# A graph layer on one core: 139 gathered columns and 15 single rows a chunk in place of 35 columns

## The chip, the cores and the metric

One core of a Trainium2 chip runs the whole program. The metric is device time in microseconds, the median of several executions; smaller is better. The figures that follow are from one profiled execution (its span is 4845.3 us, its own time 4847.12 us) unless they are called a median.

## The reference

A message-passing layer over 12500 nodes (48 features) and 400000 edges (32 features), the edges sorted by their target `dst`:

```python
h = jnp.maximum(_layernorm(x, axis=-1), 0.0)
x_i, x_j = h[dst], h[src]
tmp = jnp.concatenate([x_i, x_j, edge_attr], axis=1)       # 48 + 48 + 32
hid = jax.nn.relu(tmp @ W1 + b1)                            # 128 wide
msg = hid @ W2 + b2
out = x + jax.ops.segment_sum(msg, dst, num_segments=12500)
```

`dst` is sorted, `src` is random. That makes the target part of each edge's input local, and the source part a gather.

## The kernel before, in words

**Set-up** (the first 140 us or so). `node_tables` computes the normalised nodes and three tables: `tab_a` (nodes times the target rows of W1, with b1, in DRAM), `tab_b` (nodes times the source rows of W1, in DRAM, one row of 128 floats for each node), and `bt`, the transpose of `tab_b`, which stays in SBUF: 128 partitions, one column for each node.

**Chunks.** The edges are cut into 3125 tiles of 128 edges, eight tiles to a chunk, 391 chunks (`NCH`). The loop over the chunks is written out in full, and `manual_schedule` keeps each engine's instructions in the order in which the code names them. For chunk c:

- `prepare(c)`: SP loads the 80 rows of `tab_a` that the chunk's targets span (`rhs`), the edge features (`lhs`) and the targets (`row`). POOL gathers a row of `tab_b` for each edge into `gb`, one indirect DMA for each tile (`gathered_at`). There are six buffers `gb`, so POOL can run up to six chunks ahead; it then waits for DVE to have read the oldest. DVE builds two one-hot matrices, `lhs` (target by edge) and `hot` (edge by target).
- `before(c)`: PE multiplies `lhs` by `rhs` into `pre` in PSUM: the target part and the edge part of the hidden layer, eight tiles.
- `hidden(c)`: DVE adds `gb` to `pre` and writes `hid` in SBUF; ACT applies the relu.
- `fold(c)`: PE multiplies `hid` by `hot` into `p_g`; `add(c)`: DVE adds that into the running segment `seg`.

An iteration of the loop runs `prepare(c)`, `before(c-1)`, `fold(c-2)`, `turned(c-1)`, `hidden(c-1)` and `add(c-2)`. Every 12 chunks a segment is multiplied by W2 and stored.

**Columns in place of gathers.** Some tiles are not gathered by POOL. For these, ACT and DVE copy the edges' columns of `bt` one by one into a tile `gt` (128x128), each from an address that stands in a register (`columns`); PE adds the transpose of `gt` into `pre` (`turned`). The numbers come from the table `last`: `load` issues one TENSOR_LOAD for up to 32 registers. `PARTS` says which engine makes how many columns a chunk, and where their numbers lie in the table. Before the change DVE makes 3 and ACT twice 16, so 35 a chunk: a tile of 128 columns is full every 3.66 chunks, 106 tiles of 3125 in all, and 3019 tiles are left to POOL.

```python
PARTS = (
    (True, 0, 3, 1),
    (False, 3, 16, 4),
    (False, 19, 16, 20),
)
```

Of the kernel before, what the change touches and what calls it, by code (L numbers as in the profile page):

```python
# [8 lines left out]
F32 = mybir.dt.float32  # L9
I32 = mybir.dt.int32  # L10
AF = mybir.ActivationFunctionType
# [5 lines left out]
P = 128  # L17
N, D, DE, HID, E = 12500, 48, 32, 128, 400000
# [3 lines left out]
NT = E // P  # L22
T = 8
# [20 lines left out]
U8 = mybir.dt.uint8  # L44
# [3 lines left out]


COLS = 1  # L50
END = NT // T


PARTS = (
    (True, 0, 3, 1),
    (False, 3, 16, 4),
    (False, 19, 16, 20),
)
PART = sum(n for _, _, n, _ in PARTS)
BASE = 36  # L60
DVE_PARTS = sum(dve for dve, *_ in PARTS)
BEHIND = len(PARTS) - 1

BT0 = 16512
SEG0 = 121888
SEG_SIZE = 8 * L


SEG, NEXT, SEG2 = 40, 41, 42
PLACE0 = 43  # L70
WIDTH = 44
SLOTS = (NCH + 2 + P - 1) // P
MOST = 32

# [1 line left out]
def tiles_of(first, part):  # L76

    n = (END - first) * part // P
    return [first + (P * (j + 1) + part - 1) // part - 1 for j in range(n)]


BYCOLS = tiles_of(COLS, PART)
TURNED = {c: [j for j, of in enumerate(BYCOLS) if of == c] for c in set(BYCOLS)}


def turned_at(c):

    return ((), (T - 1,), (T // 2 - 1, T - 1))[len(TURNED.get(c, ()))]


def gathered_at(c):

    return [t for t in range(min(T, NT - c * T)) if t not in turned_at(c)]


EPS = 1e-5
# [151 lines left out]
def windows(nc, tc, gp, bt, ident, idx, x_t, tab_a, tab_b, dst, edge_t, w1, w2s, b2s, out_t):  # L248
# [3 lines left out]
    with ExitStack() as es:  # L252
# [5 lines left out]
        gtp = es.enter_context(tc.tile_pool(name="gtp", bufs=5))  # L258
        wp = es.enter_context(tc.tile_pool(name="wp", bufs=3))
# [12 lines left out]
        for _, _, n, at in PARTS:  # L272
# [1 line left out]
                last[:, :, at : at + n], last[:, :, at : at + n], 4, BT0,  # L274
                op0=ALU.mult, op1=ALU.add,
            )
        rows_at = slice(BASE, BASE + 1)
        nc.vector.tensor_scalar(
            last[:, :, rows_at], last[:, :, rows_at], 4 * HID, None, op0=ALU.mult
        )  # L280
        taba8 = tab_a.rearrange("n h -> (n h)").bitcast(U8)

        place = PARTS[0][3] - 1
        for a, b in ((place, SEG2), (NEXT, SEG)):
# [5 lines left out]
        nc.vector.scalar_tensor_tensor(  # L290
            last[:, :, at_place], last[:, :, at_place], 4.0, last[:, :, PLACE0 : PLACE0 + 1],
            op0=ALU.mult, op1=ALU.add,
# [8 lines left out]
            rhss.append(rhs)  # L301
        st = {}
        gts = {}

        def group(c):

# [5 lines left out]
        def numbers(c, at, n, engine):  # L312

            got = []
            for k in range(0, n, MOST):
                got += nc.values_load_multi_w_load_instructions(  # L316
                    last[c % P : c % P + 1, c // P, at + k : at + min(k + MOST, n)],
                    engines=[engine], min_val=0, max_val=1 << 23,
                    skip_runtime_bounds_check_because="numbers of nodes, and what is made of them",
                )[1]  # L320
            return got

        def node(n):
            return n.with_bounds(min_val=0, max_val=N - 1)

        regs = {}

        def load(c, part):

            dve, first, n, at = PARTS[part]  # L330
            n = max(0, min(n, len(BYCOLS) * P - ((c - COLS) * PART + first))) if c >= COLS else 0
            engine = mybir.EngineType.DVE if dve else mybir.EngineType.Activation
# [7 lines left out]
        def columns(c, part):  # L340
# [3 lines left out]
            for k, at in enumerate(regs.pop((c, part), [])):  # L344
                of, e = divmod((c - COLS) * PART + first + k, P)
                if of not in gts:
# [6 lines left out]
        def prepare(c):  # L353
            n = min(T, NT - c * T)
            at = c * CE
            base, = numbers(c, BASE, 1, mybir.EngineType.SP)
            rhs = rhss[c % 3]
            base = base.with_bounds(min_val=0, max_val=4 * HID * (N - 1))
            nc.sync.dma_start(
                rhs.bitcast(U8)[:W, :],  # L360
                taba8[bass.ds(base, 4 * HID * W)].rearrange("(w h) -> w h", w=W),
            )
            lhs = ld.tile([P, CE], F32, name="lhs")
            nc.sync.dma_start(lhs[W:K, : n * P], edge_t[:, at : at + n * P])
            row = ld.tile([W, CE], I16, name="row")
            nc.sync.dma_start(
                row[:, : n * P],
                dst[at : at + n * P].rearrange("(o e) -> o e", o=1).to_broadcast([W, n * P]),
            )
            st[c] = dict(n=n)  # L370
            gb = gp.tile([P, T, HID], F32, name="gb")
            for t in gathered_at(c):
                nc.gpsimd.indirect_dma_start(  # L373
                    out=gb[:, t, :], out_offset=None, in_=tab_b[:, :],
                    in_offset=bass.IndirectOffsetOnAxis(
                        ap=srci[:, c * T + t : c * T + t + 1], axis=0
                    ),
                )

            deg = degs[c % 3]  # L380
            nc.vector.tensor_scalar(  # L381
                lhs[:W, : n * P], row[:, : n * P], bw[:, c : c + 1], None,
                op0=ALU.is_equal, op1=ALU.add, accum_out=deg[:, :1],
            )
            load(c, 0)
            columns(c, 0)
            hot = wp.tile([P, T, W], F32, name="hot")
            nc.vector.tensor_tensor(  # L388
                hot[:, :n, :], wnum.unsqueeze(1).to_broadcast([P, n, W]),
                rel[:, c * T : c * T + n].unsqueeze(2).to_broadcast([P, n, W]), op=ALU.is_equal,  # L390
            )
            st[c].update(rhs=rhs, lhs=lhs, gb=gb, deg=deg, hot=hot)
# [18 lines left out]
        def hidden(c):  # L411
            s = st[c]
            n, pre = s["n"], s["pre"]
            h = wp.tile([P, T, HID], F32, name="hid")
            two = len(turned_at(c)) == 2
            half = T // 2

            def added(x, to):

                if not two:  # L420
                    return x[:, :to, :]
                return x.rearrange("p (b t) h -> p b t h", b=2)[:, :, : half - 1, :]

            to = n - len(turned_at(c))
            nc.vector.tensor_add(added(h, to), added(pre, to), added(s["gb"], to))  # L425
            if two:
                nc.scalar.activation(
                    h[:, half - 1 :: half, :], pre[:, half - 1 :: half, :], AF.Relu
                )
            elif to < n:  # L430
                nc.scalar.activation(h[:, to, :], pre[:, to, :], AF.Relu)  # L431
            nc.scalar.activation(added(h, to), added(h, to), AF.Relu)  # L432
            s["h"] = h

        def fold(c):
# [10 lines left out]
        def add(c):  # L446

            s = st.pop(c)
            k = group(c)[0] % 2
            of = SEG0 + k * SEG_SIZE  # L450
            at = s["base"].with_bounds(
# [37 lines left out]
        with tc.manual_schedule():  # L489
            for c in range(NCH + 2):  # L490
                if c < NCH:
                    prepare(c)
                if c >= NCH:
                    load(c, 0)
                    columns(c, 0)
                for part in range(1, DVE_PARTS - 1):
                    load(c, part)
                    columns(c, part)
                if 0 <= c - 1 < NCH:
                    before(c - 1)  # L500
                if 0 <= c - 2 < NCH:
                    fold(c - 2)
                if 0 <= c - 1 < NCH:
                    turned(c - 1)

                g, k = group(c - 2)
                if k == GQ - 3 or c == NCH - 1:
                    segment_load(g)
                if g > 0 and k < L // BLK:
                    segment_sum(g - 1, k, BLK)  # L510
                if g > 0 and k == STORE:
                    segment_store(g - 1, L)
                columns(c, DVE_PARTS)
                for part in range(DVE_PARTS + 1, BEHIND):
                    load(c, part)
                    columns(c, part)
                if 0 <= c - 1 < NCH:
                    hidden(c - 1)
                if DVE_PARTS > 1:
                    load(c, DVE_PARTS - 1)  # L520
                for part in range(BEHIND, len(PARTS)):
                    load(c, part)
                    columns(c, part)
                load(c + 1, DVE_PARTS)
                if 0 <= c - 2 < NCH:
                    add(c - 2)
                    if k == GQ - 1:
                        segment_next(g)
                if DVE_PARTS > 1:
                    columns(c, DVE_PARTS - 1)  # L530
                if c == NCH + 1:
                    segment_sum(g, 0, END_L)
                    segment_store(g, END_L)

                if c < PIECES:
                    s = slice(c * PIECE, (c + 1) * PIECE)
                    nc.sync.dma_start(out_t[:, s], x_t[:, s])
# [337 lines left out]
```

## Time and profile before

| | us |
|---|---|
| median of 3 runs (4817.93 to 4830.65) | 4821.73 |
| the profiled execution, its own time | 4847.12 |
| its span | 4845.3 |
| PE busy, 14064 matrix multiplications | 2962.1 |
| POOL busy (3019 gathers among it) | 2895.0 |
| ACT busy, 12976 instructions | 1944.3 |
| DVE busy, 3366 instructions | 1534.8 |

No engine is busy for two thirds of the span. The share of the DMA engines is about a fifth throughout, and the granted TensorE clock has a mean of 0.614. In the profile, "issue" as a reason for idle time means that the engine waited for nothing that the profile shows. A wait for several semaphores is put down to the one that came last.

### The profile page before, as it was taken

Reading aid. Unit: us, or ns where it says so; the run is one execution under the profiler, and the core shown is the slowest. Engines: PE = TensorE matmul, PEld = TensorE weight load, DVE = VectorE, ACT = ScalarE, POOL = GpSimd, SP = SyncE. Lnnn points to the kernel's source line nnn. Section 1 sums busy time; section 2 is a strip of 40 time slices with the busy share of each in tenths; the row PEclk is TensorE's granted clock in tenths of the full one; section 3 lists DMA queues with packets and bytes.
Section 4 is the critical chain, followed back from the end, with each engine's and each line's share of the span. In section 5 each row is a group of like instructions: output and inputs, shape, how many; then the busy total and the mean of one; then the engine's idle time right before and its main releaser. Section 6 shows DMA issues by size and latency. Waiting matters only on the chain. (4 is left out here: it accounts for less than half of the span.)

```text
span 4845.3 us, 55629 instructions
## 1 busy us (share of the span) xinstructions
PE 2962.1 (61%) x14064; PEld 2628.5 (54%) x14064; DVE 1534.8 (32%) x3366; ACT 1944.3 (40%) x12976; POOL 2895.0 (60%) x3047
## 2 busy tenths in 40 slices
PE   5565565555667555665556757666566655665656
PEld 3555564455556555655555656555455555554545
DVE  4333323332333232333323333332233332323333
ACT  3344343443334343443443444343344343434443
POOL 5466565565656566665656666656666665656663
PEclk7756656666555655556656565655655566656566
DMA  3422222222222222222222222222222222222222
GB/s 123 145 72 75 75 71 72 73 73 72 75 68 77 72 73 71 76 73 71 76 71 73 77 73 75 73 71 75 73 72 76 72 74 72 76 69 76 74 71 60
DMA packets 199966, 367.73 MB, mean 76 GB/s; under 512 B 69362, under 2 KB 101636, under 8 KB 198356
## 3 DMA queue, kind: packets, MB, share of 16 engines
q0 software_dynamic: 96640, 198.07, 16.4%
q1 hardware_dynamic: 102736, 165.92, 11.5%
q8 instruction: 115, 1.88, 0.2%
q14 instruction: 215, 1.76, 0.1%
q10 hardware_dynamic: 260, 0.10, 0.0%
HBM read 344.35 MB, written 22.07 MB: 76 GB/s over the span
## 5 line engine op out<-in xcount | busy, mean ns | idle before, releaser
L373 POOL DMA_INDIRECT gb<-tab_b,srci x3019 | 2873.3, 952 | 1898.0 <-DVE seg L455 953.0
L351 ACT COPY gt<-bt 128x1 f32 x12404 | 1495.6, 188 | 1985.4 <-issue 1957.3
L400 PE MATMUL pre<-rhs,lhs 112*128 112x128 f32 x6250 | 1357.6, 386 | 866.3 <-issue 655.1
L400 PEld LDWEIGHTS pre<-rhs,lhs 112*128 112x128 f32 x6250 | 1240.2, 292 | 1052.9 <-issue 849.9
L440 PE MATMUL p_g<-hot,hid 128*128 128x80 f32 x6250 | 1210.5, 366 | 691.2 <-ACT hid L432 312.9
L440 PEld LDWEIGHTS p_g<-hot,hid 128*128 128x128 f32 x6250 | 1156.3, 280 | 742.8 <-ACT hid L432 351.3
L425 DVE TENSOR_TENSOR hid<-pre,gb 128x1024 f32<-128x1024 f32 (+1 forms) x391 | 461.4, 1180 | 1727.0 <-issue 1357.5
L432 ACT ACTIVATE hid<-hid 128x1024 f32<-128x1024 f32 (+1 forms) x391 | 400.3, 1024 | 423.3 <-DVE hid L425 318.2
L381 DVE TENSOR_SCALAR_CACHE_REDUCE lhs<-row,bw 80x1024 f32<-80x1024 int16 x391 | 495.4, 1267 | 9.3 <-DMA row<-in_dst 9.3
L455 DVE TENSOR_TENSOR seg<-seg,p_g 128x160 f32 x391 | 122.4, 313 | 977.1 <-remote 824.1
L388 DVE TENSOR_TENSOR hot<-wnum,rel 128x640 f32<-128x640 f32 x391 | 316.1, 809 | 0.0
L443 PE MATMUL p_g<-ident,deg 80*128 80x80 f32 x782 | 213.4, 356 | 139.1 <-issue 138.8
L443 PEld LDWEIGHTS p_g<-ident,deg 80*128 80x128 f32 x782 | 181.1, 278 | 111.8 <-issue 111.4
L483 DVE TENSOR_TENSOR xseg<-xseg,p_f 48x512 f32<-48x512 f32 (+1 forms) x67 | 45.3, 676 | 497.6 <-remote 291.2
L431 ACT ACTIVATE hid<-pre 128x128 f32<-128x128 f32 x106 | 29.4, 278 | 390.0 <-DVE hid L425 273.8
L409 PE MATMUL pre<-ident,gt 128*128 128x128 f32 x212 | 70.1, 399 | 106.0 <-issue 96.1
L409 PEld LDWEIGHTS pre<-ident,gt 128*128 128x128 f32 x212 | 51.7, 282 | 108.8 <-issue 98.5
L482 PE MATMUL p_f<-seg,b2s 1*48 1x512 f32 (+1 forms) x134 | 98.0, 810 | 11.8 <-issue 11.8
L481 PE MATMUL p_f<-seg,w2s 128*48 128x512 f32 (+1 forms) x134 | 98.0, 815 | 11.3 <-issue 10.0
L351 DVE COPY gt<-bt 128x1 f32 x1164 | 103.0, 141 | 0.0
L482 PEld LDWEIGHTS p_f<-seg,b2s 1*48 1x48 f32 x134 | 13.4, 139 | 92.7 <-issue 91.8
L471 DVE MEMSET seg<- 128x944 f32 x64 | 54.1, 845 | 9.3
(66 smaller groups left out, 327.3 us busy)
## 6 DMA issues: line engine op xcount, KB each, us to landing
row<-in_dst SPq DMA_DIRECT2D x390, 160.0 KB
lhs<-in_edge_t SPq DMA_DIRECT2D x390, 128.0 KB
gb<-tab_b,srci POOLq DMA_INDIRECT x3019
rhs<-tab_a SPq DMA_DIRECT2D x391, 40.0 KB
xseg<-in_x_t SPq DMA_DIRECT2D x33, 192.0 KB
out_x<-xseg SPq DMA_DIRECT2D x33, 192.0 KB
tab_b<-tab SPq DMA_DIRECT2D x3, 1280.0 KB
tab_a<-tab SPq DMA_DIRECT2D x3, 1280.0 KB
```

Of the source, the lines that this page charges most:

```text
L351: copy(gts[of][:, e : e + 1], bt8[:, bass.ds(at, 4)].bitcast(F32))
L373: nc.gpsimd.indirect_dma_start(out=gb[:, t, :], out_offset=None, in_=tab_b[:, :], in_offset=bass.IndirectOffsetOnAxis(ap=srci[:, c * T + t ...
L381: nc.vector.tensor_scalar(lhs[:W, : n * P], row[:, : n * P], bw[:, c : c + 1], None, op0=ALU.is_equal, op1=ALU.add, accum_out=deg[:, :1],)
L388: nc.vector.tensor_tensor(hot[:, :n, :], wnum.unsqueeze(1).to_broadcast([P, n, W]), rel[:, c * T : c * T + n].unsqueeze(2).to_broadcast([P ...
L400: nc.tensor.matmul(pre[:, t, :], s["lhs"][:K, t * P : (t + 1) * P], s["rhs"][:K, :], start=True, stop=t not in turned_at(c),)
L409: nc.tensor.matmul(st[c]["pre"][:, t, :], gts.pop(j), ident, start=False, stop=True)
L425: nc.vector.tensor_add(added(h, to), added(pre, to), added(s["gb"], to))
L432: nc.scalar.activation(added(h, to), added(h, to), AF.Relu)
L440: nc.tensor.matmul(p_g[:, 0, :], s["h"][:, t, :], s["hot"][:, t, :], start=t == 0, stop=t == n - 1)
L443: nc.tensor.matmul(p_g[:, 1, :], s["deg"], ident[:W, :W], start=True, stop=True)
L455: nc.vector.tensor_add(to, to, s["p_g"])
L482: nc.tensor.matmul(p_f[:, :n], b2s[:1, :], seg[:1, 1, s], start=False, stop=True)
```

## The change

139 columns a chunk in place of 35: DVE makes 63 of them (15, 16, 16 and 16), ACT 76 (16, 16, 16, 16 and 12). Each of these nine parts has its own TENSOR_LOAD. With 139 columns a chunk, 422 tiles are made of columns. A further 45 tiles (`BYROWS`) are made of single rows: SP copies 15 rows of `tab_b` a chunk, each by a DMA of its own of 512 bytes with an address from a register, into a tile `gs` with one partition for each edge. POOL keeps 3125 - 422 - 45 = 2658 gathers. DVE now adds `gb` (and `gs` where the chunk has such a tile) to `pre` in place in PSUM, in up to three instructions, and ACT applies one relu to all eight tiles, from PSUM into `hid`.

```diff
 PARTS = (
-    (True, 0, 3, 1),
-    (False, 3, 16, 4),
-    (False, 19, 16, 20),
+    (True, 0, 15, 1),
+    (True, 15, 16, 16),
...
+    (False, 127, 12, 128),
 )
...
+        def rows(c, nodes):
+
+            for k, n in enumerate(nodes):
+                e = (c - ROWS0) * RPART + k
+                of = BYROWS[e // P]
+                if of not in gss:
+                    gss[of] = gtp.tile([P, HID], F32, name="gs")
+                n = n.with_bounds(min_val=0, max_val=4 * HID * (N - 1))
+                nc.sync.dma_start(
+                    gss[of].bitcast(U8)[e % P : e % P + 1, :],
+                    tab8[bass.ds(n, 4 * HID)].rearrange("(o h) -> o h", o=1),
+                )
...
-            base, = numbers(c, BASE, 1, mybir.EngineType.SP)
+            m = max(0, min(RPART, len(BYROWS) * P - (c - ROWS0) * RPART)) if c >= ROWS0 else 0
+            base, *nodes = numbers(c, BASE, 1 + m, mybir.EngineType.SP)
...
-            nc.vector.tensor_add(added(h, to), added(pre, to), added(s["gb"], to))
-            if two:
-                nc.scalar.activation(
-                    h[:, half - 1 :: half, :], pre[:, half - 1 :: half, :], AF.Relu
-                )
-            elif to < n:
-                nc.scalar.activation(h[:, to, :], pre[:, to, :], AF.Relu)
-            nc.scalar.activation(added(h, to), added(h, to), AF.Relu)
+            at = single_at(c)
+            if at is None:
+                parts = [(added(pre, to), added(s["gb"], to))]
+            else:
+                runs = [(0, half - 1), (half, at)] if two else [(0, at)]
+                parts = [(pre[:, a:b, :], s["gb"][:, a:b, :]) for a, b in runs]
+                parts.append((pre[:, at, :], gss.pop(c)))
+            for of, rows in parts:
+                nc.vector.tensor_add(of, of, rows)
+            h = wp.tile([P, T, HID], F32, name="hid")
+            nc.scalar.activation(h[:, :n, :], pre[:, :n, :], AF.Relu)
...
                 if c < NCH:
                     prepare(c)
+                    rows(c, st[c].pop("rows"))
```

**ACT, one chunk in mid-program.** The rows run from one relu (L432 before, L463 after) to the next; COPY is a column, with x16 for sixteen in a row, and TENSOR_LOAD fills the registers. Before:

```order
L432 ACTIVATE hid_26634<-hid_26634 128x1024
L316 TENSOR_LOAD last_87
L351 COPY gt_26362<-bt_58 128x1 x16
L316 TENSOR_LOAD last_87
L351 COPY gt_26362<-bt_58 128x1 x16
L432 ACTIVATE hid_26787<-hid_26787 128x1024
```

After, two tiles `gt` share the chunk:

```order
L463 ACTIVATE hid_87807<-pre_87671 128x1024
L331 TENSOR_LOAD last_87
L379 COPY gt_87744<-bt_58 128x1 x16
L331 TENSOR_LOAD last_87
L379 COPY gt_87744<-bt_58 128x1 x12
L331 TENSOR_LOAD last_87
L379 COPY gt_87744<-bt_58 128x1 x9
L379 COPY gt_88217<-bt_58 128x1 x7
L331 TENSOR_LOAD last_87
L379 COPY gt_88217<-bt_58 128x1 x16
L331 TENSOR_LOAD last_87
L379 COPY gt_88217<-bt_58 128x1 x16
```

Between two relus there stand 76 columns and five register loads, where there were 32 and two.

**DVE, one chunk in mid-program**, from one one-hot `lhs` (L381 before, L410 after) to the sum into `seg`. Before:

```order
L381 TENSOR_SCALAR lhs_27657,deg0_88<-row_27659,bw_85 80x1024
L316 TENSOR_LOAD last_87
L351 COPY gt_27453<-bt_58 128x1 x3
L388 TENSOR_TENSOR hot_27683<-wnum_691,rel_84 128x640
L483 TENSOR_TENSOR xseg_27235<-xseg_27235,p_f_27704 48x512
L425 TENSOR_TENSOR hid_27724<-pre_27685,gb_27500 128x1024
L455 TENSOR_TENSOR seg1_663<-seg1_663,p_g_27694 128x2x80
```

After:

```order
L410 TENSOR_SCALAR lhs_116571,deg2_92<-row_116573,bw_85 80x1024
L331 TENSOR_LOAD last_87
L379 COPY gt_116440<-bt_58 128x1 x15
L417 TENSOR_TENSOR hot_116632<-wnum_691,rel_84 128x640
L331 TENSOR_LOAD last_87
L379 COPY gt_116440<-bt_58 128x1 x16
L331 TENSOR_LOAD last_87
L379 COPY gt_116440<-bt_58 128x1 x16
L461 TENSOR_TENSOR pre_116747<-pre_116747,gb_116051 128x896
L331 TENSOR_LOAD last_87
L486 TENSOR_TENSOR seg1_663<-seg1_663,p_g_116756 128x2x80
L379 COPY gt_116440<-bt_58 128x1 x16
```

47 columns now stand ahead of the add that frees `gb` (L425 before, L461 after), and 16 behind it; before there were 3 ahead.

**SP, one chunk in mid-program**, from the register load of one chunk to that of the next. Before:

```order
L316 TENSOR_LOAD last_87
L359 DMA rhs2_706<-tab_a_64 80x512
L364 DMA lhs_20034<-in_edge_t 32x1024
L366 DMA row_20036<-in_dst16 80x1024
L316 TENSOR_LOAD last_87
```

After:

```order
L331 TENSOR_LOAD last_87
L388 DMA rhs1_710<-tab_a_64 80x512
L393 DMA lhs_42851<-in_edge_t 32x1024
L395 DMA row_42853<-in_dst16 80x1024
L349 DMA gs_40321<-tab_b_65 1x512 x15
L331 TENSOR_LOAD last_87
```

The loads of the next chunk stand behind 15 single rows of this one.

More of the change, by code (lines that the diff above doesn't have):

```diff
@@ L50 @@
 COLS = 1
+ROWS0 = 1
 END = NT // T
 PARTS = (
-    (True, 0, 3, 1),
-    (False, 3, 16, 4),
-    (False, 19, 16, 20),
+    (True, 0, 15, 1),
+    (True, 15, 16, 16),
+    (True, 31, 16, 32),
+    (True, 47, 16, 48),
+    (False, 63, 16, 64),
+    (False, 79, 16, 80),
+    (False, 95, 16, 96),
+    (False, 111, 16, 112),
+    (False, 127, 12, 128),
 )
 PART = sum(n for _, _, n, _ in PARTS)
-BASE = 36
+BASE = 140
+RPART = 15
 DVE_PARTS = sum(dve for dve, *_ in PARTS)
-BEHIND = len(PARTS) - 1
+BEHIND = len(PARTS) - 2
 BT0 = 16512
-SEG0 = 121888
+SEG0 = 123744
 SEG_SIZE = 8 * L
-SEG, NEXT, SEG2 = 40, 41, 42
-PLACE0 = 43
-WIDTH = 44
+SEG, NEXT, SEG2 = 156, 157, 158
+PLACE0 = 159
+WIDTH = 160
 SLOTS = (NCH + 2 + P - 1) // P
@@ L82 @@
 BYCOLS = tiles_of(COLS, PART)
+BYROWS = tiles_of(ROWS0, RPART)
 TURNED = {c: [j for j, of in enumerate(BYCOLS) if of == c] for c in set(BYCOLS)}
@@ L88, in turned_at, with single_at @@
     return ((), (T - 1,), (T // 2 - 1, T - 1))[len(TURNED.get(c, ()))]
+def single_at(c):
+    return (T - 2 if c in TURNED else T - 1) if c in BYROWS else None
 def gathered_at(c):
-    return [t for t in range(min(T, NT - c * T)) if t not in turned_at(c)]
+    return [t for t in range(min(T, NT - c * T)) if t not in turned_at(c) and t != single_at(c)]
 EPS = 1e-5
@@ L276, in windows @@
             )
-        rows_at = slice(BASE, BASE + 1)
+        rows_at = slice(BASE, BASE + 1 + RPART)
         nc.vector.tensor_scalar(
@@ L280, in windows @@
         )
-        taba8 = tab_a.rearrange("n h -> (n h)").bitcast(U8)
+        tab8, taba8 = (t.rearrange("n h -> (n h)").bitcast(U8) for t in (tab_b, tab_a))
         place = PARTS[0][3] - 1
@@ L303, in windows @@
         gts = {}
+        gss = {}
         def group(c):
@@ L369, in prepare @@
             )
-            st[c] = dict(n=n)
+            st[c] = dict(n=n, rows=nodes)
             gb = gp.tile([P, T, HID], F32, name="gb")
@@ L413, in hidden @@
             n, pre = s["n"], s["pre"]
-            h = wp.tile([P, T, HID], F32, name="hid")
             two = len(turned_at(c)) == 2
@@ L839 @@
         numbers[COLS : COLS + len(cols), at : at + n] = cols[:, k : k + n]
+    in_rows = [c * T + single_at(c) for c in BYROWS]
+    rows = by_tile[in_rows].reshape(-1)
+    rows = np.pad(rows, (0, -len(rows) % RPART)).reshape(-1, RPART)
+    numbers[ROWS0 : ROWS0 + len(rows), BASE + 1 : BASE + 1 + RPART] = rows
     last = np.ascontiguousarray(numbers.reshape(SLOTS, P, WIDTH).transpose(1, 0, 2))
```

## The prediction

> **What bounds the kernel now.** I read the page's groups first, then the waits, then the time line of two chunks in mid-program, and last the busy time of stretches of it. The groups (line, engine, operation, count | busy us, mean ns of one | idle time before them and what ended it):
>
> ```profile
> L373 POOL DMA_INDIRECT gb<-tab_b,srci x3019 | 2873.3, 952 | 1898.0 <-DVE seg L455 953.0
> L351 ACT COPY gt<-bt 128x1 f32 x12404 | 1495.6, 188 | 1985.4 <-issue 1957.3
> L425 DVE TENSOR_TENSOR hid<-pre,gb 128x1024 f32<-128x1024 f32 (+1 forms) x391 | 461.4, 1180 | 1727.0 <-issue 1357.5
> L409 PE MATMUL pre<-ident,gt 128*128 128x128 f32 x212 | 70.1, 399 | 106.0 <-issue 96.1
> L351 DVE COPY gt<-bt 128x1 f32 x1164 | 103.0, 141 | 0.0
> ```
>
> The loop's stretch, without set-up and tail (from, to, length, then busy us of PE, PEld, DVE, ACT and POOL):
>
> ```profile
> 155.00:4832.00 4677.00, 2869.92 (x13742) 2565.00 (x13741) 1471.62 (x3275) 1895.33 (x12884) 2828.88 (x2972) 0.61 0.28 74
> ```
>
> 4677 / 391 = 11.96 us a chunk, and 168 us outside. The waits give two odd rows: ACT is idle for 1957 us before its columns for no reason that the profile shows, 2796 times, so 0.70 us each; and POOL waits for DVE to free a buffer `gb`.
>
> ```profile
> ACT gt L351 <- issue: 1957.3, 2796, 1.9
> POOL gb L373 <- DVE seg L455: 953.0, 217, 8.9
> ```
>
> The time line (start us, length us, engine, line) shows how the two hang together. POOL, over two chunks:
>
> ```profile
> 2002.78 0.94 POOL L373 DMA_INDIRECT gb<-tab_b,srci  x1 [4.61 <-DVE seg L455]
> 2004.03 0.95 POOL L373 DMA_INDIRECT gb<-tab_b,srci  x1 [0.30 <-issue]
> ...
> 2020.28 0.95 POOL L373 DMA_INDIRECT gb<-tab_b,srci  x1 [0.30 <-issue]
> 2025.78 0.95 POOL L373 DMA_INDIRECT gb<-tab_b,srci  x1 [4.55 <-DVE seg L455]
> ```
>
> Fifteen gathers, 1.25 us from start to start, then 4.6 us of waiting: 23.0 us for two chunks. ACT and PE's weight loads in the same time:
>
> ```profile
> 2001.09 0.93 ACT L351 COPY gt<-bt 128x1 f32 x9 [0.51 <-issue]
> ...
> 2002.55 1.06 ACT L432 ACTIVATE hid<-hid 128x1024 f32<-128x1024 f32 x1 [0.52 <-DVE hid L425]
> ...
> 2003.67 2.55 ACT L351 COPY gt<-bt 128x1 f32 x25
> ...
> 2010.68 0.19 ACT L351 COPY gt<-bt 128x1 f32 x1 [0.26 <-issue]
> ...
> 2013.51 0.19 ACT L351 COPY gt<-bt 128x1 f32 x1 [1.21 <-issue]
> 2013.52 0.19 PEld L409 LDWEIGHTS pre<-ident,gt 128*128 128x128 f32 x1 [0.28 <-issue]
> ...
> 2015.63 0.19 ACT L351 COPY gt<-bt 128x1 f32 x1 [0.52 <-issue]
> 2015.65 0.29 PEld L409 LDWEIGHTS pre<-ident,gt 128*128 128x128 f32 x1 [1.94 <-issue]
> ...
> 2023.35 0.19 ACT L351 COPY gt<-bt 128x1 f32 x1 [0.51 <-issue]
> 2024.05 1.21 ACT L351 COPY gt<-bt 128x1 f32 x12 [0.51 <-issue]
> 2024.42 1.09 DVE L425 TENSOR_TENSOR hid<-pre,gb 128x896 f32<-128x896 f32 x1 [12.00 <-remote]
> ...
> 2025.42 0.31 DVE L455 TENSOR_TENSOR seg<-seg,p_g 128x160 f32 x1
> ...
> 2025.65 1.27 DVE L381 TENSOR_SCALAR_CACHE_REDUCE lhs<-row,bw 80x1024 f32<-80x1024 int16 x1
> ```
>
> At first ACT runs 25 columns in 2.55 us, 0.10 us each with their register load. From 2010.68 it starts one instruction per 0.70 or 1.4 us, though nothing holds it, and from 2013.5 PE starts its own in the same instants. At 2024.05, 2.8 us after the last gather's end (2021.23), both run freely again; DVE's add follows at once and frees POOL. So: while gathers flow, ACT and PE have a limited number of quick starts, and after these a crawl that ends with the gathers. I call it that because I do not know its cause. ACT's busy time and its instructions in the two parts:
>
> ```profile
> 2001.00:2010.00 9.00, 6.64 (x46) 0.50 0.42 112
> 2010.00:2024.00 14.00, 3.09 (x18) 0.62 0.19 47
> ```
>
> 46 starts in 9 us, then 18 in 14 us: 1.3 per us. The next pair that I read has its first stepped start earlier:
>
> ```profile
> 1782.04 0.95 POOL L373 DMA_INDIRECT gb<-tab_b,srci  x1 [4.68 <-DVE seg L455]
> ...
> 1782.90 2.71 ACT L351 COPY gt<-bt 128x1 f32 x27
> ...
> 1786.31 0.38 ACT L351 COPY gt<-bt 128x1 f32 x3 [0.70 <-issue]
> ```
>
> 27 quick starts in the 4.3 us after the gathers begin again here; in the first pair it is 39 in 7.9 us (the 46 less nine columns and a relu that began before 2002.78, and three more before 2010.68). The bound of the kernel is this loop: gathers, crawl, late add, late buffer, next gathers.
>
> **The change part by part.** *Gathers:* 2658 / 391 = 6.80 a chunk in place of 7.72. At 1.25 us that is 8.5 us in place of 9.65. Alone, with POOL's present wait of 2.3 us a chunk, this would give 10.8 us a chunk.
>
> *ACT's columns:* 76 and one relu, so 77 starts a chunk in place of 33. Free, they need 76 x 0.10 + 1.06 = 8.7 us. They are not free while gathers flow. One chunk's gathers last 5.8 x 1.25 + 0.95 = 8.2 us, and the crawl ends 2.8 us later: 11.0 us. In these ACT has 27 to 39 quick starts (in 4.3 to 7.9 us) and for the rest 1.3 a us, so 9 to 4 more: 36 to 43, say 40. There remain 37: 36 columns at 0.10 and a relu of 1.06, 4.7 us in which no gather may flow. That makes 15.7 us a chunk. With two chunks' gathers in one go: 12.6 x 1.25 + 0.95 + 2.8 = 19.5 us with 47 to 54 starts, 103 left over, 12.2 us, together 31.7, or 15.9 a chunk. I take 15.8. The ends: if there are no quick starts at all, 14 of 77 in the 11.0 us, 63 left over, 7.3 us: 18.3 us. If the quick starts suffice for a chunk, the period is that of a single chunk's gathers as it stands in the trace now:
>
> ```profile
> 1675.64 0.95 POOL L373 DMA_INDIRECT gb<-tab_b,srci  x1 [8.88 <-DVE seg L455]
> ...
> 1688.45 0.95 POOL L373 DMA_INDIRECT gb<-tab_b,srci  x1 [3.11 <-DVE seg L455]
> ```
>
> 12.8 us. I stay near the upper of these readings, since ACT made only 33 starts in that one.
>
> *DVE's columns:* 63 in place of 3. Three take 0.27 us where one takes 0.14 (below), so 0.065 us from start to start: 4.1 us. With its other work of a chunk, the rows of 1.27, 0.08, 0.81, 1.09 and 0.31 us, that is some 7.7 us and four register loads. No row shows DVE in the crawl; it has had too few instructions. If it falls into it as ACT does, it has some 69 starts and loses as much, beside ACT. If the two wait for each other in turn, the period grows towards the upper end; 19 us is as far as I go. 47 columns now stand ahead of the add that frees `gb`, 3.1 us: hidden as long as `pre` comes later than that.
>
> *Turned tiles:* 316 more, two multiplications of 0.40 us each: 253 us, 0.65 us a chunk, in PE's idle time (PE is busy for 2870 of 4677 us). *The in-place add and the one relu* remove an ACT instruction in 106 chunks and lengthen the other; nothing, under 0.1 us a chunk either way. *Set-up* loads a larger table beside other loads: nothing, 5 us at worst by my guess.
>
> *SP's rows:* 18 DMAs a chunk in place of 3.
>
> ```profile
> 2001.22 0.33 SPq L359 DMA_DIRECT2D rhs<-tab_a  x1
> 2001.66 0.36 SPq L364 DMA_DIRECT2D lhs<-in_edge_t  x1
> ```
>
> 0.44 us from start to start, so 7.9 us of SP a chunk, below the period. Queued behind the rows stand the next chunk's `rhs`, `lhs` and `row`, for which DVE and PE wait; SP now idles for most of a chunk, so I set this at nothing, with a rival below.
>
> **The sum.** 391 x 15.8 + 168 = 6346 us of span; the profiled execution was 2 us longer than its span and 25 us above the median: 6323, rounded to 6320. The forecast's own range is 12.8 to 19 us a chunk: 5150 to 7570.
>
> **The rivals.** *Faster: the crawl does not grow with the starts.* If it comes only from long runs of gathers, or ends sooner with fewer of them, then POOL's sum holds: 10.8 us a chunk, 4370; with POOL's wait gone too, ACT's 8.7 and POOL's 8.5 us with some joint waiting, 9.5 us, 3860. For it: every engine's free sum is under 9 us. Against it: the stepped starts stand before plain copies that wait for nothing, and the free time between gathers is now 5 us for two chunks. It decides at about 75 starts of ACT within 11 us of gathers; the trace shows 43 at most.
>
> *SP becomes the bound.* Its DMAs take eight semaphores in turn, so that each waits for the one eight before it. If one takes 5.3 us from issue to landing, 18 take 12 us: no change; at 6 us 13.5, 5420. Against it: they are small.
>
> *DVE's copies hold POOL up.* If POOL stood still for each of DVE's columns, its sum would be 10.8 + 4.1 = 14.9 us, 5970. The rows for and against:
>
> ```profile
> 1806.70 1.83 DVE L471 MEMSET seg<- 128x944 f32 x2
> 1807.84 1.60 POOL L373 DMA_INDIRECT gb<-tab_b,srci  x1 [0.30 <-issue]
> ...
> 1809.73 0.08 DVE L381 DVE_READ_ACCUMULATOR lhs<-row,bw 80x1 f32 x1
> 1809.73 0.27 DVE L351 COPY gt<-bt 128x1 f32 x3
> 1809.74 0.94 POOL L373 DMA_INDIRECT gb<-tab_b,srci  x1 [0.30 <-issue]
> 1809.92 0.81 DVE L388 TENSOR_TENSOR hot<-wnum,rel 128x640 f32<-128x640 f32 x1
> ```
>
> The gather beside DVE's wide fills of SBUF takes 1.60 us, the one beside three columns 0.94 like any other. [...]
>
> **How the numbers follow.** Forecast 0.68, faster rival 0.22, SP 0.05, DVE against POOL 0.05. The range leaves out the lower half of the faster rival (0.11) and the far end of the crawl (0.06): 4300 to 7600. By 0.3%, about what a measurement of this kernel can tell from no change: faster 0.22; same 0.02, where SP or a short crawl happens to meet 11.96 us; slower 0.76.
>
> **What would show it.** Right: ACT's idle time for "issue" before its columns far above 1957 us, its starts in steps of 0.70 us while gathers flow, and POOL idle for half of each period, with DVE's add named as the releaser. DVE's columns may show the same steps. Wrong: 76 columns run in 8 us beside gathers; or POOL busy without waits; or gathers longer than 0.95 us beside DVE's columns; or SP's queue never idle while DVE waits for `row` or `gs`.

## The result, and the profile after

In the runs of the result the change makes the kernel slower: median 5245.6 us (4 runs, 5243.6 to 5253.49) against 4826.19 us (4 runs), ratio 1.0873, 95% interval 1.0851 to 1.0895. The forecast was 6320 us. The direction held, the size did not: 420 us were added, not 1500. The profiled execution of after has a span of 5244.5 us.

The groups of after (columns as before):

```profile
L379 ACT COPY gt<-bt 128x1 f32 x29509 | 3121.2, 187 | 1583.5 <-issue 1555.6
L402 POOL DMA_INDIRECT gb<-tab_b,srci x2658 | 2534.0, 953 | 2623.0 <-DVE pre L461 1331.7
L379 DVE COPY gt<-bt 128x1 f32 x24507 | 1821.8, 143 | 1673.9 <-issue 1666.2
```

DVE now has what ACT had before: idle time in which it waits for nothing. POOL's gathers are as long as they were, and POOL is idle as long as it works. The loop, then the waits (who waited for whom: us in total, times, longest):

```profile
155.00:5230.00 5075.00, 3111.74 (x14345) 2823.16 (x14346) 3096.45 (x26638) 3446.38 (x29851) 2493.36 (x2615) 0.61 0.24 64
```

```profile
DVE gt L379 <- issue: 1666.2, 2445, 2.3
ACT gt L379 <- issue: 1555.6, 2672, 4.3
POOL gb L402 <- DVE pre L461: 1331.7, 248, 51.9
...
POOL gb L402 <- DVE seg L486: 558.6, 134, 7.9
```

5075 / 391 = 12.98 us a chunk, where the forecast had 15.8. The time line of one period:

```profile
2000.87 4.18 ACT L379 COPY gt<-bt 128x1 f32 x42
...
2001.90 0.95 POOL L402 DMA_INDIRECT gb<-tab_b,srci  x1 [4.97 <-DVE pre L461]
...
2003.62 9.68 SPq L349 DMA_DIRECT2D gs<-tab_b  x15
...
2006.84 0.19 ACT L379 COPY gt<-bt 128x1 f32 x1 [0.50 <-issue]
2006.84 0.15 DVE L379 COPY gt<-bt 128x1 f32 x1 [0.50 <-issue]
...
2007.54 1.02 ACT L463 ACTIVATE hid<-pre 128x1024 f32<-128x1024 f32 x1 [0.51 <-issue]
...
2009.39 0.95 POOL L402 DMA_INDIRECT gb<-tab_b,srci  x1 [0.30 <-issue]
...
2010.37 0.19 ACT L379 COPY gt<-bt 128x1 f32 x1 [0.43 <-issue]
2010.37 0.15 DVE L379 COPY gt<-bt 128x1 f32 x1 [0.50 <-issue]
...
2011.80 2.15 ACT L379 COPY gt<-bt 128x1 f32 x21 [0.52 <-issue]
2011.80 1.24 DVE L379 COPY gt<-bt 128x1 f32 x19 [0.56 <-issue]
...
2015.80 1.10 DVE L461 TENSOR_TENSOR pre<-pre,gb 128x896 f32<-128x896 f32 x1 [2.76 <-PE pre L438]
...
2017.17 0.94 POOL L402 DMA_INDIRECT gb<-tab_b,srci  x1 [6.83 <-DVE pre L461]
```

In outline it is the loop of the prediction: seven gathers, ACT and DVE stepping by 0.70 us in the same instants, both free 1.5 us after the last gather's end, then the add and the next gathers. SP is slowed too: its fifteen rows take 9.68 us here, 8.5 us in the mean, against 5.1 us in `e6` below, a run of the same kernel in which nothing steps.

Here the add waits 2.76 us for PE, which is the rarer case. In the next period it stands behind DVE's own columns, and the gathers begin again while ACT still has 2.2 us of columns ahead of its relu:

```profile
2027.16 0.64 DVE L379 COPY gt<-bt 128x1 f32 x9 [1.20 <-issue]
...
2028.31 4.79 ACT L379 COPY gt<-bt 128x1 f32 x48 [0.41 <-issue]
2028.45 1.06 DVE L379 COPY gt<-bt 128x1 f32 x16 [0.66 <-issue]
...
2029.43 1.09 DVE L461 TENSOR_TENSOR pre<-pre,gb 128x896 f32<-128x896 f32 x1
...
2030.79 0.94 POOL L402 DMA_INDIRECT gb<-tab_b,srci  x1 [5.17 <-DVE pre L461]
...
2033.00 1.01 ACT L463 ACTIVATE hid<-pre 128x1024 f32<-128x1024 f32 x1
```

In 305 of 373 chunks in mid-program (the 13th to the 385th) DVE goes into the add within 0.2 us of its instruction before it; in 282 of these, all that PE had to deliver for it had been there for over 1 us.

### The profile page after: what moved, and what is told of

Same layout as the page of the kernel before. It is cut to its first block, busy times and chain, and to the rows that moved or that the text cites. A ratio compares the mean times of both kernels' runs of the same rounds, so it can differ in the third digit from the quotient of the medians.

```text
span 5244.5 us, 110315 instructions
## 1 busy us (share of the span) xinstructions
PE 3207.9 (61%) x14696; PEld 2890.4 (55%) x14696; DVE 3164.3 (60%) x26769; ACT 3498.4 (67%) x29975; POOL 2555.7 (49%) x2686
## 4 chain that ended last, share of the span: by engine, by line
ACT 56%; issue 29%; ACTq 4%; PE 3%; DVE 3%; another core or an unknown queue 1%; DVEq 0%
ACT gt L379 50%; ACT hid L463 7%; ACTq L331 4%; PE p_g L471 1%; DVE gt L379 1%; DVE pre L461 1%; PE pre L429 0%; DVEq L331 0%; DVE lhs L410 0%; PE p_f L513 0%; PE p_f L512 0%; DVE hot L417 0%; PE pre L438 0%; PE p_g L474 0%
## 5 line engine op out<-in xcount | busy, mean ns | idle before, releaser
L379 ACT COPY gt<-bt 128x1 f32 x29509 | 3121.2, 187 | 1583.5 <-issue 1555.6
L402 POOL DMA_INDIRECT gb<-tab_b,srci x2658 | 2534.0, 953 | 2623.0 <-DVE pre L461 1331.7
L379 DVE COPY gt<-bt 128x1 f32 x24507 | 1821.8, 143 | 1673.9 <-issue 1666.2
L471 PE MATMUL p_g<-hot,hid 128*128 128x80 f32 x6250 | 1348.1, 404 | 1881.1 <-ACT hid L463 880.9
L471 PEld LDWEIGHTS p_g<-hot,hid 128*128 128x128 f32 x6250 | 1270.6, 310 | 1970.2 <-ACT hid L463 928.2
L429 PE MATMUL pre<-rhs,lhs 112*128 112x128 f32 x6250 | 1272.4, 389 | 15.6 <-DMA gs<-tab_b 15.6
L461 DVE TENSOR_TENSOR pre<-pre,gb 128x896 f32<-128x896 f32 (+4 forms) x400 | 417.4, 1044 | 154.9 <-issue 111.2
L410 DVE TENSOR_SCALAR_CACHE_REDUCE lhs<-row,bw 80x1024 f32<-80x1024 int16 x391 | 494.4, 1265 | 7.7 <-DMA row<-in_dst 7.7
L463 ACT ACTIVATE hid<-pre 128x1024 f32<-128x1024 f32 x391 | 396.4, 1014 | 66.7 <-issue 41.6
L438 PE MATMUL pre<-ident,gt 128*128 128x128 f32 x844 | 287.6, 444 | 86.8 <-remote 53.6
L438 PEld LDWEIGHTS pre<-ident,gt 128*128 128x128 f32 x844 | 215.2, 313 | 96.8 <-remote 59.1
```

The lines of the kernel that those rows point to most:

```text
L379: copy(gts[of][:, e : e + 1], bt8[:, bass.ds(at, 4)].bitcast(F32))
L402: nc.gpsimd.indirect_dma_start(out=gb[:, t, :], out_offset=None, in_=tab_b[:, :], in_offset=bass.IndirectOffsetOnAxis(ap=srci[:, c * T + t ...
L410: nc.vector.tensor_scalar(lhs[:W, : n * P], row[:, : n * P], bw[:, c : c + 1], None, op0=ALU.is_equal, op1=ALU.add, accum_out=deg[:, :1],)
L429: nc.tensor.matmul(pre[:, t, :], s["lhs"][:K, t * P : (t + 1) * P], s["rhs"][:K, :], start=True, stop=t not in turned_at(c),)
L438: nc.tensor.matmul(st[c]["pre"][:, t, :], gts.pop(j), ident, start=False, stop=True)
L461: nc.vector.tensor_add(of, of, rows)
```

## The experiments

Beside all experiments, on five chips, the kernel before itself took 3846 to 3855 us, and not 4818 to 4832 as in the runs of the result: there are two conditions, and the second group below (`e5`, `e6`) shows in what they differ.

**Gathers left out, or made plain.** In `e1` and `e2` POOL gathers only in the first six chunks; the later chunks add those six buffers again.

```diff
-            gb = gp.tile([P, T, HID], F32, name="gb")
-            for t in gathered_at(c):
+            if c < 6:
+                gb = gp.tile([P, T, HID], F32, name="gb")
+                gbs.append(gb)
+            gb = gbs[c % 6]
+            for t in range(T) if c < 6 else ():
```

> The kernel after with POOL's gathers left out from the seventh chunk on (the sums read old rows of gb); all columns, single rows and multiplications stay. Theory (the steps of 0.70 us come only while gathers flow): ACT's columns run 0.10 us apart throughout, the loop takes ACT's 76 x 0.10 + 1.06 and some waiting, 8.7 to 9.5 us a chunk, 3550 to 3900 us in all, and ACT's idle time for issue falls below 300 us. Rival (the steps come from the number of instructions itself): steps remain, over 4800 us.

> The kernel before with POOL's gathers left out from the seventh chunk on. Theory: no steps; PE's 36 multiplications and weight loads a chunk (about 7 us) and the chain from DVE's add over the relu to PE bound it: 7 to 8.5 us a chunk, 2900 to 3500 us, less than the kernel after without gathers. Rival (steps come with instructions): 4300 us or more.

In `e3` and `e4` each gather is a plain DMA of 128 neighbouring rows, so the wrong rows but as many bytes:

```diff
-                nc.gpsimd.indirect_dma_start(...)
+                first = (c * T + t) % NR * P
+                nc.gpsimd.dma_start(gb[:, t, :], tab_b[first : first + P, :])   # e4: nc.sync
```

> The kernel before with each gather replaced by a plain DMA of 128 neighbouring rows of tab_b, still issued by POOL, same bytes and same buffers (other rows than the reference needs). If the steps come with transfers that POOL issues, of whatever kind: steps as before, 4500 to 5000 us unless POOL is quicker with plain DMAs. If they come with the indirect form: no steps, 3000 to 3900 us.

> The same plain DMAs, issued by SP. If any transfer of these bytes brings the steps: steps as before, 4500 to 5000 us. If only transfers that POOL issues bring them: no steps, SP's 10.7 DMAs at 0.43 us are hidden, and the time is near that of the kernel before without gathers, 2900 to 3600 us.

Measured, one run each: 3521.36, 2022.21, 2023.39 and 2475.18 us. The rows of `e1`, `e2`, and POOL's of `e3`:

```profile
L380 ACT COPY gt<-bt 128x1 f32 x29509 | 2885.7, 188 | 70.6 <-issue 32.5
```

```profile
L352 ACT COPY gt<-bt 128x1 f32 x12404 | 1223.4, 187 | 25.3 <-issue 9.8
```

```profile
L374 POOL DMA_DIRECT2D gb<-tab_b x3019 | 1589.9, 535 | 360.7 <-DVE seg L451 176.1
```

No crawl in any. But the kernel before took 3849.5 us beside them, 970 us less than in the result, so these runs could not show that the gathers cause it. They price two other things: without gathers the changed kernel is bound by ACT at 3520 us, and the kernel before drops to 2022 us. `e2` came out far below the 2900 us at which its expectation began, so much more of the kernel before hangs on the gathers than was thought. In `e4` SP's queue heads the chain that ended last (36%): DVE idles for 564 us until a `row` lands that stands behind the gathers' rows in it.

**Both kernels again.** `e5` and `e6` are the kernels before and after, unchanged.

> The kernel before, unchanged, for a trace of it beside the experiments, because it took 3849.5 us beside the runs without gathers and 4821 to 4830 us earlier. If the cost of a gather's companions is a fixed step of 0.70 us per instruction, then the step must be shorter or rarer where the kernel takes 3850 us: ACT's idle time of the cause issue, 1957 us in the first trace, should be about 970 us less. If instead the gathers themselves were shorter there, POOL's 0.95 us each should be near 0.65 us and ACT's issue idle nearly the same.

> The changed kernel, unchanged, beside the same kernel before. If the crawl is a loss of starts in proportion to the instructions that fall into it, the ratio to the kernel before stays above 1.05 wherever both run: about 4185 us beside 3850 us. If where the kernel before takes 3850 us the crawl is nearly gone, the time is what ACT needs for its own work, near the 3521 us that this kernel takes without gathers, and the change is a gain.

Measured: `e5` 3847.8 us; `e6` 3538.62 us, ratio **0.9203** (0.9173 to 0.9233) to 3850.91 us, the median of 13 runs of the kernel before beside it. Here the same change is a gain of 8%. Before again, groups and waits:

```profile
L373 POOL DMA_INDIRECT gb<-tab_b,srci x3019 | 2854.2, 945 | 940.9 <-issue 862.9
...
L351 ACT COPY gt<-bt 128x1 f32 x12404 | 1227.2, 187 | 42.7 <-issue 13.8
```

```profile
POOL gb L373 <- issue: 862.9, 2831, 0.3
...
ACT gt L351 <- issue: 13.8, 57, 0.6
```

ACT's idle time for "issue" is 13.8 us in place of 1957.3. POOL hardly waits for a buffer (once, 1.1 us); a gather follows a gather at 0.945 + 0.30 = 1.25 us, and 3019 x 1.25 = 3774 us. That leaves 72 us of the span of 3846.1 us for set-up, tail and a few single waits. This kernel is bound by POOL, where the first trace showed a loop over the crawl. After again:

```profile
L402 POOL DMA_INDIRECT gb<-tab_b,srci x2658 | 2523.5, 949 | 914.0 <-issue 725.8
L379 ACT COPY gt<-bt 128x1 f32 x29509 | 2886.1, 187 | 72.0 <-issue 31.9
L379 DVE COPY gt<-bt 128x1 f32 x24507 | 1621.6, 142 | 243.1 <-issue 239.8
```

Each operation is as long as in the first pair (gathers 953 and 949 ns, ACT's copies 187 and 187, DVE's 143 and 142), and 76 columns run in one go, in 7.55 us, beside flowing gathers:

```profile
2005.39 0.94 POOL L402 DMA_INDIRECT gb<-tab_b,srci  x1 [0.30 <-issue]
2005.42 7.55 ACT L379 COPY gt<-bt 128x1 f32 x76
...
2006.64 0.95 POOL L402 DMA_INDIRECT gb<-tab_b,srci  x1 [0.30 <-issue]
```

Without gathers this kernel took 3521 us, with them 3539: the gathers are hidden, and ACT, 93% busy, is the bound. Of the two expectations, a ratio above 1.05 wherever both run and a gain where the crawl is gone, the first fell.

**Part by part.** `e7` is after without SP's rows, POOL gathering their 45 tiles (`BYROWS = []`). `e8` is before with only the in-place add and the one relu:

```diff
-            nc.vector.tensor_add(added(h, to), added(pre, to), added(s["gb"], to))
-            ... the relu of the turned tiles, the relu of the others
+            nc.vector.tensor_add(added(pre, to), added(pre, to), added(s["gb"], to))
+            nc.scalar.activation(h[:, :n, :], pre[:, :n, :], AF.Relu)
```

> Leaves out SP's 15 single rows per chunk; the 45 tiles that they filled are gathered by POOL again. If SP's 15 added issues, which go at 0.65 us each in the crawl and take 9.7 us of a 13 us chunk, bind nothing, the time stays within 2% of the changed kernel's (45 gathers more are 45 x 0.95 = 43 us of POOL, which is idle half the time). If SP sets the chunk's length, the chunk shrinks by the 9.7 us of issues down to the next bound, and the time falls by over 10%.

> The kernel before with only the third part of the change: the add of the gathered rows in place in PSUM, and one relu for all tiles of the chunk in place of one for the gathered and one for the turned tiles. The prediction put this part at nothing: within 1% of the kernel before. If the add in PSUM or the relu from PSUM holds the next chunk's matmuls back, the time rises by over 1%; if the one start fewer on ACT and the shorter relu come off the chain, it falls by about 391 x 0.3 = 100 us at the most.

Measured: `e7` 3520.17 us (0.9134, 0.9116 to 0.9153), half a per cent under `e6`; `e8` 3850.72 us (1.0002, 0.9993 to 1.0012). The rows bring nothing while ACT binds (they cost that half per cent); the in-place add and the one relu are worth nothing, as forecast, here.

**Other splits of the columns.** `e9`: `PARTS` with 67 columns on DVE and 72 on ACT. `e10`: 63 and 32, no rows.

> The changed kernel with four of ACT's columns moved to DVE: 67 and 72. Where the other engines do not crawl (the kernel before at 3850 us), POOL's 1.25 us a gather sets a chunk at 6.80 x 1.25 = 8.50 us and ACT's own work falls from 8.6 to 8.2 us a chunk: 391 x 8.50 + 72 = 3395 us, at most 3450, if ACT was what bound the changed kernel there. If the chain through the add and the relu binds and not ACT's sum, the time stays at 3525 to 3550. Where they crawl (the kernel before at 4820 us), the two starts that are moved change nothing: both engines start one instruction per step, 5150 to 5350 us.

> The changed kernel with the 32 columns a chunk on ACT that the kernel before has, 63 on DVE, and without SP's single rows: DVE's part of the change alone. 95 columns a chunk fill 290 tiles, so POOL gathers 2837. Where nothing crawls, POOL's cadence of 1.25 us sets the time: 2837 x 1.25 + 72 = 3618 us, within 40. Where they crawl, the theory that starts inside the gathers' stretch are what counts, on whichever engine they are, puts it between the two kernels, 4900 to 5150 us; the rival that only ACT's starts count puts it below the kernel before, 4450 to 4700.

Measured: `e10` 3632.83 us (0.9437, 0.9421 to 0.9453), within the 40 us: POOL's cadence, and POOL's gathers hold 51% of the chain that ended last. DVE's columns, with the in-place add, bring 216 us by themselves. `e9` missed: 3586.98 us (0.9315, 0.9287 to 0.9343), slower than `e6`, not 3395 to 3450. A sum of ACT's work does not give the time of such a kernel. Its four more columns on DVE stand behind one chunk's add and so ahead of the next one's. DVE's waits in `e9`, and ACT's for the add:

```profile
DVE gt L379 <- issue: 240.1, 401, 2.3
DVE seg L486 <- DVE pre L461: 96.0, 299, 0.7
DVE xseg L514 <- PE p_f L513: 59.2, 28, 8.9
...
ACT hid L463 <- DVE pre L461: 216.7, 168, 9.5
```

The first row is mostly the pause for a register load (0.57 us, once a chunk), the second DVE's wait for its own add. In the loop DVE waits for another engine for some 60 us in all, its add follows its instruction before it at once in all of the 373 chunks, and ACT waits for that add (116 us in `e6`). So DVE's own work binds `e9`.

`e11`: 63 on DVE and 61 on ACT with the rows kept. `e12`: 53 and 71 with the rows.

```diff
 e12:
-    (True, 47, 16, 48),
-    (False, 63, 16, 64),
+    (True, 47, 6, 48),
+    (False, 53, 16, 54),
 ...
```

> The changed kernel with its 63 columns on DVE and 15 single rows by SP, and 61 columns on ACT in place of 76: the 15 single rows pay for 15 columns. As many tiles are kept from POOL as without the rows and with 76 (8 - 139/128 = 6.91 gathers a chunk). Where nothing crawls: if ACT's sum of 8.6 us a chunk is what bound the changed kernel, ACT falls to 7.2 us and POOL's 6.91 x 1.25 = 8.64 us bind, 391 x 8.64 + 72 = 3450 us; if DVE's order of work (its columns ahead of the add, on which ACT's relu waits) is what binds, as moving four columns to DVE suggests, ACT's relief buys nothing: 3500 to 3560. Where the engines crawl, 5000 to 5250.

> The same 124 columns and 15 single rows, with DVE relieved rather than ACT: 53 on DVE, 71 on ACT. Where nothing crawls: if DVE's order of work binds, this is the faster of the two, 3450 us, POOL's bound of 6.91 gathers at 1.25 us; if ACT's sum binds (71 x 0.098 + 1.1 = 8.1 us, under POOL's 8.64), it is also near 3450 to 3480, and the other kernel of this call tells the two apart. Where the engines crawl, 5000 to 5250.

Measured: `e11` **3475.19 us** (0.9022, 0.9007 to 0.9037), the best of all here, 63 us under `e6`; POOL heads its chain with 35%. `e12` 7272.76 us, ratio 1.89. Its trace is no crawl: no engine steps, and ACT stands still ahead of each sixteen columns, during the load of its registers. First `e12`, then `e6`:

```profile
2003.47 1.58 ACT L379 COPY gt<-bt 128x1 f32 x16 [2.46 <-issue]
...
2007.52 1.58 ACT L379 COPY gt<-bt 128x1 f32 x16 [2.46 <-issue]
```

```profile
2003.02 1.58 ACT L379 COPY gt<-bt 128x1 f32 x16 [0.18 <-issue]
```

The load of sixteen registers takes 3.48 us in `e12` (median) and 1.03 us in `e6`. In `e12` ACT's numbers begin at words 54, 70, 86, 102 and 118 of a row of the table, in all others at multiples of four. `e13` is `e12` with only that place moved (`(False, 53, 16, 54)` to `(False, 53, 16, 56)`, and so on). `e14` is `e11` without the rows.

> The kernel with 53 columns on DVE and 71 on ACT, with nothing changed but the place of ACT's numbers in the table: they begin at words 56, 72, 88, 104 and 120 of a row rather than 54, 70, 86, 102 and 118. In the 7273 us run ACT's loads of sixteen registers took 3.48 us each, and 1.05 us where they begin at word 64. If the place (a word that is a multiple of four) is the cause, the loads take 1.05 us again and the time is 3450 to 3500 us, POOL's bound of 6.91 gathers at 1.25 us a chunk. If the slow stepping of the first pair of traces is the cause, the place changes nothing and it stays near 7270.

> 63 columns on DVE and 61 on ACT, as in the kernel of 3475 us, without SP's 15 single rows: 124 of 128 columns turn into 7.03 gathers a chunk. If POOL's cadence binds at this split, the rows are worth 0.117 gathers x 1.25 us x 391 = 57 us, and the time is 391 x 8.79 + 72 = 3509 to 3535 us. If DVE's order of work binds (the rows split its add in two), the time is 3475 or less.

Measured: `e13` 3530.79 us (0.9158, 0.9139 to 0.9178), its loads 1.03 us. The group of ACT's columns in `e12` and in `e13`:

```profile
L379 ACT COPY gt<-bt 128x1 f32 x27548 | 2747.8, 187 | 4031.0 <-issue 4021.0
```

```profile
L379 ACT COPY gt<-bt 128x1 f32 x27548 | 2732.7, 187 | 248.9 <-issue 223.6
```

Two words of place were 3742 us. What is left of ACT's idle time in `e13` is one pause a chunk, 0.53 us, 387 times, behind the part of seven columns, which is too short (0.75 us in the time line of `e12`) to hide the next load (1.03 us). `e14` 3521.83 us (0.9146, 0.9131 to 0.9161): the rows are worth 47 us once ACT does not bind; 57 had been worked out. Their gathers against the rule from `e5` (72 us and 1.25 us a gather):

| | gathers | 72 + 1.25 x gathers | span |
|---|---|---|---|
| `e5` (before; the 72 is from it) | 3019 | 3846 | 3846.1 |
| `e10` 63 + 32 | 2837 | 3618 | 3631.7 |
| `e14` 63 + 61 | 2749 | 3508 | 3520.6 |
| `e11` 63 + 61, rows | 2704 | 3452 | 3475.5 |
| `e13` 53 + 71, rows | 2704 | 3452 | 3532.9 |
| `e7` 63 + 76 | 2703 | 3451 | 3525.3 |
| `e6` 63 + 76, rows | 2658 | 3395 | 3524.3 |
| `e9` 67 + 72, rows | 2658 | 3395 | 3583.7 |

The rule holds within 24 us up to 61 columns on ACT. Past that something else binds: ACT's sum in `e6` and `e7` (93% busy), DVE's in `e9`. In `e13` ACT's columns are half of the chain that ended last, ACT is busy for 88% and pauses for 0.53 us a chunk; that this is all that holds it is not shown. From `e9`, four columns of 0.065 us fewer on DVE, 391 x 0.26 = 102 us, would put DVE's bound at 63 columns near 3482 us, by estimate: `e11`, at 3475.5, stands about where POOL and DVE are equal.

## Why the prediction was right in direction and wrong in size

This account holds for the condition of the first pair, in which both kernels crawl.

- *The loop.* Right in outline: gathers, crawl, late add, next gathers. POOL waits for DVE's add: 2.3 us a chunk before, 12.98 - 8.50 = 4.5 us after, and that is more than the 1.15 us that 0.92 gathers fewer save. But one sign of being right did not come: ACT's idle time for "issue" fell from 1957 to 1556 us, where it was to go far above. DVE has 1666 us of it beside.
- *Gathers, 6.80 a chunk at 1.25 us.* Right (1.25 us apart above).
- *Starts of ACT in a stretch: 36 to 43, say 40.* About right. From the first gather until ACT runs freely again:

```profile
2001.90:2011.80 9.90, 5.88 (x45) 0.63 0.30 82
2011.80:2017.17 5.37, 5.20 (x53) 0.50 0.20 47
2017.17:2027.15 9.98, 5.19 (x40) 0.95 0.23 58
```

45 and 40 instructions of ACT in two stretches, and the free part between them. Over the 384 stretches of one chunk's gathers (five to seven) it is 44 starts on average, 43 columns and the relu. That the trace of before shows "43 at most" is wrong: of ACT's starts within 11 us of a first gather 43 is the median there, over 222 stretches, and up to 54, once 66, occur.

- *The step that failed is the stretch and what is left after it.* "The crawl ends 2.8 us later" was read from the end of fifteen gathers; after one chunk's it ends 1.4 us after the last (mean of the 384), so the stretch is 9.7 us and not 11.0. What is left is 3.4 us and not 4.7 (together 13.1; the first chunks, which wait for no buffer, bring the mean to 12.98). The relu's 1.06 us was charged to it; in 96% of the chunks the relu starts inside the next stretch, in 80% before ACT's first step there, 2.3 us (median) behind the first gather. 1.3 + 1.1 us, with the starts more than reckoned (0.3 us) and what was rounded up (0.1 us), make the 2.8 us a chunk between 15.8 and 12.98, and 391 x 2.82 = 1103 us is the whole miss (6346 - 5244.5).
- *Whose work fills the rest.* The prediction ended the time without gathers with ACT's last columns and relu, and called DVE's 47 columns ahead of the add hidden as long as `pre` comes later. In three of four chunks `pre` comes earlier (the 282 of 373 above). The 3.4 us are then DVE's: 2.2 us from its release to the add, mostly its remaining columns, 1.0 us for the add, 0.2 us to the next gather. ACT fills the same time and hardly waits either, but what it has not done goes on beside the next gathers. Which of the two would hold the loop without the other is not shown: no run moved columns between them in the crawl.
- *The nearer number.* The period of a single chunk's gathers that already stood in the trace of before, 12.8 us, would have come closest. It was set aside because ACT had made only 33 starts in it; that it comes so near may be luck, since DVE had only three columns there.
- *DVE in the crawl.* Right that it falls into it: 2445 waits of 0.68 us. It does so in the same instants as ACT and loses them beside it. What its columns cost is the point above.
- *SP's rows, set at nothing.* In the crawl fifteen take 8.5 us in the mean, 0.57 us each and not 0.44, in a 13 us chunk. DVE waits for `row` for 7.7 us in the whole run, so no cost of them shows, but the loop without the rows was not run in the crawl, so this is argued and not shown.
- *DVE's copies hold POOL.* This rival fell: gathers beside 63 columns take 953 ns, beside three 952.
- *The in-place add, the one relu.* Nothing: shown without the crawl (`e8`), not in it.

The larger fault lies under all of these: the prediction took the crawl for a property of the kernel. It is one of the condition in which both traces were taken. Without it the kernel before is bound by POOL's cadence, each tile kept from POOL is worth 1.25 us until ACT binds, and the sign turns: 0.9203. The prediction's faster rival named that case (POOL's 8.5 and ACT's 8.7 us, "some joint waiting", 3860), and still put it 320 us too high.

What makes the crawl stays open. One more thing differs between the pairs: the trace of before holds 21,318 records of semaphore updates in the first condition and 74,190 in `e5`, for the same 55,629 instructions; of the 52,872 missing, 51,212 tell of a DMA that landed. Many waits of the first pair are put down to "remote", and none of the 57 longest groups of waits in `e5` is; that the missing records make them so is an inference:

```profile
DVE seg L455 <- remote: 824.1, 93, 16.6
```

So records are missing from the trace of before, and in both traces of the first pair engines step in the same instants, in after down to SP's register moves (699 of 6,223 take 0.6 to 0.8 us, none over 0.1 us in `e6`, median 0.03). That one comes from the other is a guess that no run here shows: the crawl did not come back on any of the five chips, and none of these kernels brought it about. On which chip the first pair ran is not on record, so a difference of the chip is a rival that nothing here excludes.

## What to carry to other kernels

Before a row such as "waits for nothing, 0.70 us, 2796 times" becomes the base of a forecast, run the unchanged kernel again elsewhere: an idle time that hangs on the condition of the runs can turn the sign of a change. Where a loop is bound by a count of equal operations, its cadence times the count is a good rule (within 24 us for three kernels here, with the 72 us from a fourth) until another engine's work passes it; moving work then pays only as far as that point, which was 61 columns on ACT and not 76, and 63 on DVE and not 67. The engine with the longest work is not always the one that holds a loop: look which instruction ends the others' wait, and what stands ahead of it in its own queue. And a tail or a period is taken from the case in the trace that looks like the kernel to come, here one chunk's gathers and not two.

## What the runs showed of the hardware

- The load of sixteen registers from SBUF takes 1.03 us where the numbers begin at word 56 or 64 of a table row (`e13`, `e6`) and 3.48 us where they begin at word 54 (`e12`); for one kernel that was 3531 against 7273 us. Words 54, 70, 86, 102 and 118 were slow (118 with seven registers: 1.60 us, against 1.00 us at word 120); no other place off a multiple of four was tried with so many registers.
- An indirect gather of 128 rows holds POOL for 0.945 us and the next follows at 1.25 us (`e5`), a plain DMA of as many bytes for 0.535 us (`e3`).
- With the gathers gone (`e2`), or made plain and still issued by POOL (`e3`), the kernel before takes 2022 and 2023 us with a granted clock of 0.98, against 3848 us and 0.665 with them (`e5`).
